# Row scores of the second layer spread by TensorE for every pair, instead of by a 32x32 turn and a way through DRAM, with new step lists

## The chip, the core and the metric

The kernel runs on one core of a Trainium2 chip. A core has five engines with queues of their own: TensorE (PE, with its weight loads shown apart as PEld), VectorE (DVE), ScalarE (ACT), GpSimd (POOL) and SyncE (SP), which here issues nearly all DMAs. [...] The metric is the device time of one execution in microseconds; lower is better.

## The reference

128 graphs of 128 nodes with 512 features go through two layers, all in f32. The first is attention with 8 heads whose scores are weighed with the adjacency; the second is a graph attention layer whose softmax runs over the rows:

```python
h = jnp.maximum(_layernorm(x, axis=-1), 0.0)
q, k, v = (proj(Wq, bq), proj(Wk, bk), proj(Wv, bv))
scores = jnp.einsum('bhqd,bhkd->bhqk', q, k) * SCALE * (adj + adj)[:, None, :, :]
ctx = jnp.einsum('bhqk,bhkd->bhqd', jax.nn.softmax(scores, axis=-1), v)
x = x + jnp.einsum('bse,fe->bsf', ctx, Wo) + bo

h = jnp.maximum(_layernorm(x, axis=-1), 0.0)
Wh = jnp.einsum('bsi,io->bso', h, W)
e = jax.nn.leaky_relu(Wh @ a[:OUT_F, :] + jnp.swapaxes(Wh @ a[OUT_F:, :], 1, 2), negative_slope=0.2)
attention = jax.nn.softmax(jnp.where(adj > 0.5, e, -9e15), axis=1)
x = x + jax.nn.elu(jnp.einsum('bst,bto->bso', attention, Wh))
```

In the kernel the second layer works on the transposed adjacency, so that its softmax runs along the free dimension. One of the two terms of e is then a number for each partition, and the other, the row score, a number for each column, which has to stand in all 128 partitions. How this row gets there is what the change touches.

## The kernel before, in words

**Tiling.** The graphs are taken in 64 pairs p, and two pairs make a group g. The products for q, k and v are made for a group at once, all others for a pair. Every product with a 512x512 weight is done with seven block products in place of eight (PRODUCTS, as in Strassen's method); that is why sums of blocks are made on VectorE: of weights (`weight_sum`, once), of the hidden rows (`hidden_sum`, steps hs0 to hs3), of the context (cs0 to cs3) and of the gathered rows (gs0 to gs3). Every f32 matmul shows as two passes in the profile, a transpose as one.

**Steps.** The work of a pair is cut into steps with short names, a table of functions for each pair (`steps`, line 680). Nothing is reordered by a scheduler: three lists written into the kernel say which step of which pair is issued next, and each engine runs its instructions in that order. HEAD (line 577) is the start, with `name@pair`; ORDER (line 601) is run through for p = 3 to 59, with `name:lag` for the pair p - lag; TAIL (line 611) is the end, with pairs counted from the last. A step that was done, or that a pair does not have, is passed over. The steps that matter here, with engine and line:

- U1 to U11 (PE, L258): block products of q, k, v for the next group, ten for an even pair and eleven for an odd one; F (ACT, L270, L275) and A (DVE, L279) take them out of PSUM.
- sca, scb (PE, L320): scores of graph a and b of the pair, two PSUM banks each; ata0, ata1, atb0, atb1 (DVE, L327): their weighing, which frees a bank each; mx (DVE, L334), ex (ACT, L339), rc (DVE, L343), nm*a*/nm*b* 0 to 3 (ACT, L348): the softmax; fl (DVE, L355), bl and pl (SP, L359, L365): the weights are turned in 32x32 blocks, written to DRAM and fetched back with the blocks in place.
- pca, pcb (PE, L388) with the pair before: context; pea, peb (ACT, L395) take it out. o0 to o6 (PE, L299) and od (DVE, L402): output product, added to x. sh (DVE, L234) adds a constant row to x first.
- st0, st1 (DVE, L165, L166), pw (POOL, L172, L173), nm (DVE, L412, writes nmr), h20, h21 (ACT, L418): norm and relu of the second layer.
- d00, d10, d01, d11 (DVE, L425): the two score columns of each graph, sums along the rows.
- px (DVE, L439), pd (SP, L444), pv (SP, L449): the row score, see below. wm (DVE, L455), pr (ACT, L460), m1 (DVE, L464), e1 (ACT, L469), sw (DVE, L474, L475): mask, leaky relu and softmax of the second layer.
- g0, g1 (PE, L481): rows gathered with these weights; ge0, ge1 (ACT, L487) take them out; w0 to w6 (PE, L299), zc (ACT, L495), wd (DVE, L499): product with W; ez (ACT), fa, fb (DVE, L511, L515), so (SP): elu, sum and store. The last pair does this by quarters (qe, qa, qb, qs).
- t0, t1 (DVE, L165), s0 (POOL), f0 (SP), lT (SP), hd0, hd1 (DVE, L222, L224): norm and relu of the first layer, ahead of time. For the first four pairs tp0, tp1 (PE, L197) transpose the normalised rows hn (DVE, L190) instead. lx, l0, la, lt (SP) load x (twice), the adjacency and its transpose.
- W and L steps (DVE, SP): sums and loads of the weights, in two halves each; ccp, ccd, ccs, cch make the constant row c (PE, L531: 16 matmuls of one column), sup and sua the rows u (PE, L553: transposes of a column broadcast over 128 columns).

**PSUM.** All PSUM tiles come from one pool of eight banks (`ps1`, line 57). A tile gets a bank when its first matmul is issued, and this matmul waits until the last reader of the tile that had the bank is done.

**The row score before.** For pairs 0 to 61, d writes the score of graph i into column 0 of `src_sb[:, i, :]` (128 x 2 x 32, zeros elsewhere). px turns this in 32x32 blocks on VectorE, so that the scores stand in rows 0, 32, 64, 96; pd writes these rows to DRAM; pv reads them back to all partitions, into the tile w; wm works there. For pairs 62 and 63, near the end, pb (`scores1`, line 429) is used: one transpose on TensorE for each graph, with the column broadcast over 128 columns as its input, into a PSUM tile that wm reads.

Of the kernel before, what the change touches and what calls it, by code (L numbers as in the profile page):

```python
# [10 lines left out]
OP = mybir.AluOpType  # L11
# [13 lines left out]
def kernel(  # L25
# [133 lines left out]
    def row_stats(src, name, soon=False):  # L159

        mv = small.tile([P, 2, 2], F32, name=name)

        def stats(i):
            st = small.tile([P, nc.vector.BN_STATS_DIM], F32, name="st", bufs=1)
            nc.vector.bn_stats(st, src[:, i, :])  # L165
            nc.vector.bn_aggr(mv[:, i, :], st)  # L166
            if soon:
                nc.vector.tensor_scalar_add(mv[:, i, 1:2], mv[:, i, 1:2], EPS)  # L168

        def power():  # L170
# [199 lines left out]
    src_sb = const.tile([P, 2, Q], F32, name="src1")  # L370
    nc.gpsimd.memset(src_sb, 0.0)


# [35 lines left out]
    def centre1(p):  # L409
        mv = l1s[p][0]  # L410
        nmr = small.tile([P, 2], F32, name="nmr", bufs=2)
# [10 lines left out]
    def dot1(p, i, k):  # L422
        h2, ws = h1s[p]
        junk = work.tile([P, E], F32, name="junk")
        nc.vector.scalar_tensor_tensor(  # L425
            junk, h2[:, i, :], 1.0, u_sb[:, k, :], op0=OP.mult, op1=OP.mult, accum_out=ws[:, i, 1:2] if k else src_sb[:, i, 0:1]
        )

    def scores1(p):

        pb = ps1.tile([P, 2, S], F32, name="pb", tag="ps1")
        for i in range(2):
            nc.tensor.transpose(pb[:, i, :], src_sb[:, i, 0:1].to_broadcast([P, P]), ident)
        pbs[p] = pb

    def turn_scores1(p):

        wts[p] = work.tile([P, 2, S], F32, name="w", bufs=2)
        nc.vector.transpose(wts[p][:, 0, 0 : 2 * Q], src_sb.rearrange("p b q -> p (b q)"))  # L439

    def send_scores1(p):
        pbs[p] = dram.tile([2, P], F32, name="row1")
        rows = wts[p][0:P:Q, 0, 0 : 2 * Q].rearrange("j (b q) -> j b q", q=Q)
        nc.sync.dma_start(pbs[p].rearrange("b (j q) -> j b q", q=Q), rows)  # L444

    def spread_scores1(p):
        r = pbs[p]
        pbs[p] = wts[p]
        nc.sync.dma_start(wts[p].rearrange("p b s -> p (b s)"), r.rearrange("b p -> (b p)").partition_broadcast(P))  # L449

    def mask1(p):

        if p not in wts:
            wts[p] = work.tile([P, 2, S], F32, name="w", bufs=2)
# [7 lines left out]
    def maxima1(p):  # L462
        l1s[p] = small.tile([P, 2], F32, name="nmx1", bufs=2), small.tile([P, 2], F32, name="sums1", bufs=2)
# [7 lines left out]
    def normalise1(p):  # L471
        w, (_, sums) = wts[p], l1s.pop(p)
        rs = small.tile([P, 2], F32, name="rs1", bufs=1)
# [100 lines left out]
    def listed(text, mark):  # L574
# [3 lines left out]
        lx@0 lx@1 Lq1@0 Lq0@0 lx@2 Lk0@0 Lk1@0 Lv0@0 t1@-5 Lo0@0 t0@-5 pp@0 hn0@0 hn1@0 tp0@0 t0@-4 tp1@0 ev0@0 ev1@0  # L578
        t1@-4 U6@-2 Wq0@0 pp@1 Wq1@0 t1@-3 U8@-2 hn0@1 l0@-2 Wq2@0 Lv1@0 hn1@1 tp0@1 Lo1@0 U3@-1 Lw1@0 t0@-3 ev0@1 Lu@0
        Wq3@0 pp@2 tp1@1 hn1@2 U5@-1 ev1@1 hn0@2 F6@-2 Wk0@0 hs0@-3 F3@-1 U1@-2 Wk1@0 hs1@-3 hs2@-3 U10@-2 tp0@2 F10@-2  # L580
        U7@-1 t1@-2 t0@-2 U2@-1 Wv0@0 F7@-1 pp@3 Wk3@0 F1@-2 A8@-2 ev0@2 U9@-1 hn0@3 Wv1@0 hn1@3 hs3@-3 tp0@3 l0@-1
        tp1@2 Wv2@0 la@-1 U3@-2 ev1@2 Lw0@0 ev0@3 lt@0 F9@-1 tp1@3 F2@-1 ccp@0 F3@-2 ev1@3 U1@0 ccd@0 t0@-1 t1@-1 U4@-2
        Wo0@0 l0@0 s0@-1 cu10@0 U5@-2 Wv3@0 A5@-1 U4@-1 hs0@-1 U10@-1 U1@-1 F10@-1 F4@-1 ccs@0 A2@-1 cch@0 sca@0 Wk2@0
        scb@0 ata0@0 ata1@0 U6@-1 mxa@0 hs1@-1 exa2@0 U3@1 t1@0 F5@-2 exa3@0 A6@-1 U6@0 A5@-2 F1@0 Wo1@0 rca1@0 t0@0
        U9@-2 F6@0 l0@1 s0@0 exa1@0 f0@0 exa0@0 U3@0 A9@-2 nma3@0 Wo2@0 nma2@0 rca0@0 cu01@0 U10@0 nma1@0 nma0@0 hs2@-1
        F3@1 U8@0 fla@0 Ww0@0 bla@0 U8@-1 atb0@0 la@0 atb1@0 mxb@0 U5@1 A8@0 exb2@0 A9@-1 pla@0 U2@-2 exb0@0 A5@1 exb1@0
        sh@0 F10@0 U11@-1 exb3@0 rcb1@0 U7@-2 nmb3@0 A11@-1 rcb0@0 t0@1 t1@1 U2@1 F7@-2 nmb1@0 cu11@0 l0@2 s0@1 nmb2@0
        f0@1 U7@1 F3@0 lT@0 cu00@0 nmb0@0 lT@1 sca@1 A2@-2 flb@0 scb@1 pca@0 F7@1 ata0@1 blb@0 ata1@1 F2@1 U5@0 mxa@1
        hs3@-1 exa0@1 U9@1 t1@2 exa1@1 Ww2@0 plb@0 exa3@1 t0@2 U1@1 exa2@1 hd0@0 s0@2 F9@1 la@1 U4@1 l0@3 pea@0 rca0@1
# [239 lines left out]
```

## Time and profile before

| | |
|---|---|
| runs | 2363.86, 2363.51, 2363.39, 2364.44 us; median 2363.69 |
| profiled execution | 2363.86 us, its span 2362.10 us (1.76 us lie around the span) |
| TensorE clock granted, mean | 0.997 |
| busy: DVE, ACT, POOL | 2001.1, 1457.1, 256.6 us |
| DMA | 314.06 MB, 133 GB/s mean |
| two pairs in the steady part | 72.65 us (the scores' first matmul at 1012.16 and at 1084.81) |

The profile's page gives each engine's busy time and share, the span in slices, the DMA queues, the chain of work that ended last, and groups of equal instructions with mean duration and the idle time before them. Other views are asked of the trace: the waits (who waited for whom, total us, times, longest), one tile's instructions, and the instructions in order of time (start, us, engine, line, operation, output and input, count, and in brackets the idle time before and what ended it). A run of equal matmuls is shown merged; its length reaches to the modelled end of the last, which overlaps the next run.

### The profile page before, as it was taken

The numbers are of one execution on the slowest core, as the hardware profiler recorded it, in microseconds if no ns is written. First come the engines' busy times: TensorE is split into PE (matmuls) and PEld (weight loads), VectorE is DVE, ScalarE is ACT, GpSimd is POOL, SyncE is SP. The second block draws the span as 40 slices with busy tenths as digits, with TensorE's granted clock in tenths as the row PEclk, the third lists the DMA queues.
The fourth block names the chain that finished last, engine by engine and source line by source line (L and its number), as shares of the span: only waits on it lengthen the run. The fifth ranks groups of instructions, "written<-read, shape, count | busy, mean of one in ns | idle before, by whom it ended". The sixth has DMA issues, their size and how long they took to land.

```text
span 2362.1 us, 41114 instructions
## 1 busy us (share of the span) xinstructions
PE 2336.9 (99%) x14184; PEld 2065.4 (87%) x14184; DVE 2001.1 (85%) x4113; ACT 1457.1 (62%) x4815; POOL 256.6 (11%) x320
## 2 busy tenths in 40 slices
PE   9999999999999999999999999999999999999998
PEld 7888888888888888888888888888888888888886
DVE  5888888888888888888888888888888888888888
ACT  2656666666566665666666666656666565665775
POOL 1101101111101011011110111110101101110000
PEclk9999999999999999999999999999999999999999
DMA  4444454454444544434545345444454443443332
GB/s 156 142 114 148 124 151 115 125 158 126 140 133 121 150 132 135 139 114 144 148 126 150 117 123 159 125 143 130 125 148 134 132 139 113 145 147 119 117 119 94
DMA packets 267352, 314.06 MB, mean 133 GB/s; under 512 B 24200, under 2 KB 192136, under 8 KB 267144
## 3 DMA queue, kind: packets, MB, share of 16 engines
q1 hardware_dynamic: 263112, 311.31, 43.8%
q8 instruction: 112, 1.84, 0.3%
q0 software_dynamic: 1920, 0.13, 0.2%
q14 instruction: 96, 0.79, 0.1%
q10 hardware_dynamic: 2112, 0.01, 0.0%
HBM read 210.51 MB, written 100.85 MB: 132 GB/s over the span
## 4 chain that ended last, share of the span: by engine, by line
PE 89%; DVE 4%; POOL 3%; ACT 3%; issue 1%; DMA 0%; POOLq 0%; SPq 0%; ACTq 0%; DVEq 0%
PE acc_a L258 26%; PE row_a L299 23%; PE acc_c L258 12%; PE row_c L299 8%; PE acc_b L258 7%; PE pc L388 5%; PE sc L320 3%; PE pg L481 3%; POOL mv L173 2%; ACT h L418 2%; DVE st L165 2%; POOL mv L172 1%; DVE x L402 1%; DVE v L279 1%; ACT gT L487 1%
## 5 line engine op out<-in xcount | busy, mean ns | idle before, releaser
L339 ACT ACTIVATE at<-at,nmx 128x128 f32<-128x128 f32 x1024 | 396.1, 391 | 18.0 <-DVE nmx L334 17.9
L299 PE MATMUL row_a<-wo,cxT 128*128 128x256 f32 x1280 | 328.4, 379 | 0.3 <-DVE cxT L153 0.3
L348 ACT ACTIVATE at<-at,rs 128x128 f32<-128x128 f32 x1024 | 323.6, 392 | 3.8 <-DVE rs L343 3.7
L299 PE MATMUL row_a<-w,gT 128*128 128x256 f32 x1280 | 319.4, 380 | 2.9 <-DVE z L499 1.7
L172 POOL TENSOR_SCALAR mv<-mv 128x2 f32<-128x2 f32 x124 | 79.2, 639 | 2031.1 <-DVE mv L166 2008.8
L299 PEld LDWEIGHTS row_a<-w,gT 128*128 128x128 f32 x1280 | 242.3, 190 | 37.9 <-DVE z L499 2.6
L299 PEld LDWEIGHTS row_a<-wo,cxT 128*128 128x128 f32 x1280 | 242.6, 190 | 34.3 <-DVE cxT L153 0.6
L402 DVE TENSOR_TENSOR x<-row_a,x 128x256 f32<-128x256 f32 x320 | 135.0, 422 | 147.3 <-PE row_a L299 144.7
L495 ACT COPY z<-row_a 128x256 f32<-128x256 f32 x256 | 94.4, 369 | 210.9 <-PE row_a L299 210.8
L275 ACT ACTIVATE kT<-acc_a,bk 128x256 f32<-128x256 f32 x256 | 106.5, 467 | 176.9 <-PE acc_a L258 173.7
L327 DVE SCALAR_TENSOR_TENSOR at<-sc,adj 128x512 f32<-128x512 f32 x256 | 165.0, 685 | 42.4 <-PE sc L320 39.9
L339 ACT ACTIVATION_READ_ACCUMULATOR at<-at,nmx 128x1 f32 x1024 | 193.8, 189 | 0.0
L418 ACT ACTIVATE h<-x,nmr,mv 128x512 f32<-128x512 f32 x128 | 97.5, 808 | 151.0 <-DVE nmr L412 148.7
L165 DVE BATCH_NORM_STATS2 st<-x 128x6 f32<-128x512 f32 x256 | 176.0, 687 | 7.3 <-DMA x<-in_x 5.0
L275 ACT ACTIVATE qT<-acc_a,bq 128x256 f32<-128x256 f32 x256 | 106.1, 466 | 123.2 <-PE acc_a L258 123.2
L425 DVE SCALAR_TENSOR_TENSOR junk<-h,u 128x512 f32<-128x512 f32 x256 | 173.1, 676 | 0.6
L355 DVE STREAM_TRANSPOSE tr<-at 128x1024 f32<-128x1024 f32 x128 | 158.7, 1240 | 7.0 <-PE pc L388 2.7
L334 DVE TENSOR_REDUCE nmx<-at 128x8 f32<-128x1024 f32 x128 | 156.2, 1220 | 4.3
L481 PEld LDWEIGHTS pg<-w,h 128*128 128x128 f32 x1024 | 133.3, 192 | 6.6 <-ACT z L495 0.2
L388 PE MATMUL pc<-aT,v 128*64 128x128 f32 x2048 | 127.5, 277 | 11.0 <-ACT gT L487 10.9
L173 POOL TENSOR_TENSOR mv<-mv,mhalf 128x2 f32<-128x2 f32 x128 | 130.6, 1020 | 32.8 <-DVE mv L168 22.5
L481 PE MATMUL pg<-w,h 128*128 128x128 f32 x1024 | 134.1, 275 | 0.0
(130 smaller groups left out, 4863.4 us busy)
## 6 DMA issues: line engine op xcount, KB each, us to landing
blocks<-tr SPq DMA_DIRECT2D x128, 512.0 KB, 6.5
aT<-blocks SPq DMA_DIRECT2D x512, 128.0 KB, 2.9
x<-in_x SPq DMA_DIRECT2D x123, 512.0 KB, 4.8
out<-x SPq DMA_DIRECT2D x63, 512.0 KB, 4.1
hA<-in_xT SPq DMA_DIRECT2D x120, 256.0 KB, 3.6
mr<-rows SPq DMA_DIRECT2D x60, 256.0 KB, 4.1
adj<-in_adj SPq DMA_DIRECT2D x64, 128.0 KB, 4.0
adjT<-in_adjT SPq DMA_DIRECT2D x64, 128.0 KB, 3.8
```

The lines of the kernel that those rows point to most:

```text
L165: nc.vector.bn_stats(st, src[:, i, :])
L173: nc.gpsimd.tensor_tensor(mv[:, :, 1], mv[:, :, 1], mhalf.to_broadcast([P, 2]), OP.pow)
L258: nc.tensor.matmul(acc[:, m, :], lhsT, rhs, start=fresh and m == 0 and c == 0, stop=c == 1, skip_group_check=True)
L275: nc.scalar.activation(dst(t, f)[:, m, :], a[:, m, :], AF.Identity, bias=bias[:, j : j + 1])
L299: nc.tensor.matmul(acc, left[:, la, c, :], w[:, wb, c, :], start=n in (0, 3) and c == 0, stop=c == 1, skip_group_check=True)
L327: nc.vector.scalar_tensor_tensor(ats[b][0][:, k * C : (k + 1) * C, :], scs[b][k], QSCALE, adjs[p][:, i : i + 1, :].to_broadcast([P, C, S]) ...
L339: nc.scalar.activation(at[:, j, :], at[:, j, :], AF.Exp, bias=nmx[:, j : j + 1], accum_out=sums[:, j : j + 1])
L348: nc.scalar.activation(at[:, j, :], at[:, j, :], AF.Copy, scale=rs[:, j : j + 1])
L355: nc.vector.transpose(trs[b], at.rearrange("p h (j k) -> p j h k", k=Q))
L388: nc.tensor.matmul(pc[s * D : (s + 1) * D, j, :], vs[b // G][:, b % G, head * D : (head + 1) * D], aT[:, :, s * C + j, :], start=True, sto ...
L425: nc.vector.scalar_tensor_tensor(junk, h2[:, i, :], 1.0, u_sb[:, k, :], op0=OP.mult, op1=OP.mult, accum_out=ws[:, i, 1:2] if k else src_sb ...
L481: nc.tensor.matmul(pg[:, c, :], h1s[p][0][:, i, c * P : (c + 1) * P], wts[p][:, i, :], start=True, stop=True)
```

## The change

All pairs now do what the last two did: d writes both score columns into the small tile `ws`, pb makes the row of each graph by a transpose on TensorE, and wm reads it from PSUM. px, pd and pv go, with `src_sb`. The small tiles st, nmr, nmx1, sums1 and rs1, which had one or two buffers, get the pool's three. The three step lists are replaced by others: the same steps, but for px, pd, pv and pb, in another order. Among what is ordered otherwise: at the start the three loads of x come ahead of the weights' loads, the statistics of pairs 0 and 1 and of half of pair 2 ahead of the first hn, and all four transposes of pairs 0 and 1 ahead of the first product; in ORDER ge1 stands ahead of h20 and h21, st1 after fb, and g0 and g1 between products o of the pair after.

```diff
         def stats(i):
-            st = small.tile([P, nc.vector.BN_STATS_DIM], F32, name="st", bufs=1)
+            st = small.tile([P, nc.vector.BN_STATS_DIM], F32, name="st")
...
-    src_sb = const.tile([P, 2, Q], F32, name="src1")
-    nc.gpsimd.memset(src_sb, 0.0)
...
-        nmr = small.tile([P, 2], F32, name="nmr", bufs=2)
+        nmr = small.tile([P, 2], F32, name="nmr")
...
         nc.vector.scalar_tensor_tensor(
-            junk, h2[:, i, :], 1.0, u_sb[:, k, :], op0=OP.mult, op1=OP.mult, accum_out=ws[:, i, 1:2] if k else src_sb[:, i, 0:1]
+            junk, h2[:, i, :], 1.0, u_sb[:, k, :], op0=OP.mult, op1=OP.mult, accum_out=ws[:, i, k : k + 1]
         )
 
     def scores1(p):
+        ws = h1s[p][1]
 
         pb = ps1.tile([P, 2, S], F32, name="pb", tag="ps1")
         for i in range(2):
-            nc.tensor.transpose(pb[:, i, :], src_sb[:, i, 0:1].to_broadcast([P, P]), ident)
+            nc.tensor.transpose(pb[:, i, :], ws[:, i, 0:1].to_broadcast([P, P]), ident)
         pbs[p] = pb
 
-    def turn_scores1(p):
+    def mask1(p):
 
         wts[p] = work.tile([P, 2, S], F32, name="w", bufs=2)
-        nc.vector.transpose(wts[p][:, 0, 0 : 2 * Q], src_sb.rearrange("p b q -> p (b q)"))
-
-    def send_scores1(p):
...
-    def spread_scores1(p):
...
-    def mask1(p):
-
-        if p not in wts:
-            wts[p] = work.tile([P, 2, S], F32, name="w", bufs=2)
         nc.vector.scalar_tensor_tensor(wts[p], adjTs.pop(p), 0.5, pbs.pop(p), op0=OP.is_le, op1=OP.subtract)
...
-        l1s[p] = small.tile([P, 2], F32, name="nmx1", bufs=2), small.tile([P, 2], F32, name="sums1", bufs=2)
+        l1s[p] = small.tile([P, 2], F32, name="nmx1"), small.tile([P, 2], F32, name="sums1")
...
-        rs = small.tile([P, 2], F32, name="rs1", bufs=1)
+        rs = small.tile([P, 2], F32, name="rs1")
...
     HEAD = """
-        lx@0 lx@1 Lq1@0 Lq0@0 lx@2 Lk0@0 Lk1@0 Lv0@0 t1@-5 Lo0@0 t0@-5 pp@0 hn0@0 hn1@0 tp0@0 t0@-4 tp1@0 ev0@0 ev1@0
-        t1@-4 U6@-2 Wq0@0 pp@1 Wq1@0 t1@-3 U8@-2 hn0@1 l0@-2 Wq2@0 Lv1@0 hn1@1 tp0@1 Lo1@0 U3@-1 Lw1@0 t0@-3 ev0@1 Lu@0
-        Wq3@0 pp@2 tp1@1 hn1@2 U5@-1 ev1@1 hn0@2 F6@-2 Wk0@0 hs0@-3 F3@-1 U1@-2 Wk1@0 hs1@-3 hs2@-3 U10@-2 tp0@2 F10@-2
-        U7@-1 t1@-2 t0@-2 U2@-1 Wv0@0 F7@-1 pp@3 Wk3@0 F1@-2 A8@-2 ev0@2 U9@-1 hn0@3 Wv1@0 hn1@3 hs3@-3 tp0@3 l0@-1
-        tp1@2 Wv2@0 la@-1 U3@-2 ev1@2 Lw0@0 ev0@3 lt@0 F9@-1 tp1@3 F2@-1 ccp@0 F3@-2 ev1@3 U1@0 ccd@0 t0@-1 t1@-1 U4@-2
...
+        lx@0 lx@1 lx@2 Lk0@0 Lv0@0 Lq0@0 Lv1@0 Lk1@0 t1@-5 Lq1@0 lt@0 t1@-4 t0@-5 t0@-4 pp@0 t1@-3 pp@1 hn0@0 l0@-2
+        hn1@0 tp0@0 Lw0@0 hn0@1 Lo1@0 tp1@0 hn1@1 ev0@0 Lw1@0 tp0@1 ev1@0 Lo0@0 tp1@1 la@-1 ev0@1 U2@-2 Lu@0 ev1@1 U3@-1
+        U8@-2 F3@-1 Wv0@0 t0@-3 U6@-2 Wv1@0 pp@2 hs0@-3 hs1@-3 U5@-1 Wk0@0 Wk1@0 Wq0@0 U1@-2 Wk3@0 hs2@-3 Wq1@0 U7@-1
+        F1@-2 hn0@2 hn1@2 Wq2@0 tp0@2 F7@-1 t1@-2 U3@-2 F6@-2 A2@-2 A8@-2 U10@-2 t0@-2 hs3@-3 pp@3 U9@-1 F10@-2 F3@-2
+        Ww0@0 A5@-1 U2@-1 F9@-1 hn0@3 ev0@2 hn1@3 Wv2@0 l0@-1 tp1@2 F2@-1 Wv3@0 ccp@0 Wk2@0 tp0@3 U10@-1 cu11@0 U4@-1
+        F10@-1 t1@-1 Wq3@0 tp1@3 F4@-1 U5@-2 t0@-1 ev1@2 ev0@3 l0@0 s0@-1 ev1@3 sca@0 scb@0 ata0@0 ata1@0 U8@-1 cu00@0
...
     ORDER = """
-        U1:0 fa:4 ge0:3 pw:2 hs1:1 fb:4 g1:3 nm:2 lT:0 so:4 sca:0 h20:2 scb:0 h21:2 ata0:0 ge1:3 ata1:0 pca:1 mxa:0
-        pcb:1 pea:1 d00:2 F1:0 U11:1 exa1:0 A6:1 A8:1 U2:0 exa0:0 d10:2 exa3:0 t0:0 px:2 exa2:0 gs0:3 rca0:0 w0:3 pd:2
-        A11:1 A10:8 A1:8 nma1:0 rca1:0 w1:3 gs1:3 t1:0 nma2:0 gs2:3 o0:1 s0:0 zc0:3 nma0:0 lx:1 wd1:3 U3:0 nma3:0 hs3:1
-        d01:2 fla:0 o1:1 F3:0 peb:1 w2:3 atb0:0 bla:0 atb1:0 w3:3 zc2:3 mxb:0 F2:0 la:-1 w4:3 pv:2 gs3:3 lt:2 U5:0 zc4:3
-        cs0:1 cs2:1 cs1:1 F5:0 sh:1 pla:0 exb3:0 U4:0 exb2:0 exb0:0 rcb1:0 od0:1 l0:-1 U7:0 od1:1 exb1:0 f0:-1 wd4c:3
-        F8:-8 A5:0 nmb3:0 A2:0 F4:0 U8:0 nmb2:0 A3:3 rcb0:0 d11:2 F11:-4 nmb0:0 cs3:1 nmb1:0 A7:-9 o2:1 w5:3 od2:1 wm:2
-        U6:0 A4:-4 flb:0 zc5:3 pr:2 m1:2 blb:0 hd0:0 e1:2 w6:3 F6:0 o4:1 F7:0 o3:1 od4:1 wd6:3 U9:0 od4c:1 sw:2 F9:0
-        plb:0 hd1:0 ez:3 o5:1 hs2:0 hs0:0 o6:1 od5:1 U10:0 A9:0 st0:1 od6:1 g0:2 st1:1 F10:0
+        U1:0 A9:1 F10:1 pw:2 so:4 hs2:1 A1:8 ge1:3 F8:-4 gs0:3 w0:3 nm:2 w1:3 zc0:3 sca:0 F11:1 h20:2 wd1:3 gs2:3 scb:0
+        h21:2 A4:8 ata0:0 ata1:0 pca:1 lx:1 hs1:1 pcb:1 mxa:0 pea:1 F1:0 U11:1 gs1:3 lT:0 exa1:0 A6:1 d00:2 U2:0 exa3:0
+        d10:2 exa0:0 A8:1 d01:2 exa2:0 U3:0 rca0:0 d11:2 peb:1 nma0:0 A11:1 w2:3 rca1:0 F2:0 cs0:1 cs1:1 nma1:0 w3:3
+        zc2:3 pb:2 nma2:0 U4:0 wm:2 nma3:0 cs2:1 A2:0 pr:2 gs3:3 F3:0 o0:1 fla:0 o1:1 atb0:0 bla:0 w4:3 A7:-9 A3:-1 m1:2
+        f0:0 atb1:0 lt:1 U5:0 zc4:3 mxb:0 la:0 e1:2 sh:1 o3:1 wd4c:3 pla:0 w5:3 od0:1 od1:1 U6:0 zc5:3 F5:0 A10:7 A5:0
+        exb2:0 sw:2 exb3:0 w6:3 exb0:0 rcb1:0 o2:1 wd6:3 exb1:0 cs3:1 g0:2 od2:1 nmb2:0 hs3:1 rcb0:0 nmb3:0 o4:1 fa:3
+        nmb1:0 U7:0 nmb0:0 t1:0 ge0:2 od4:1 od4c:1 g1:2 F7:0 flb:0 ez:3 o5:1 blb:0 F6:0 o6:1 od5:1 F4:0 st0:1 U9:0 t0:0
+        F9:0 od6:1 s0:0 U8:0 hd0:0 plb:0 hd1:0 U10:0 hs0:0 fb:3 st1:1 l0:-1
     TAIL = """
...
-        nmb3@-1 od2@-2 so@-4 ge1@-3 flb@-1 o4@-2 ge0@-3 o3@-2 od4@-2 blb@-1 cs3@-2 gs0@-3 o5@-2 pea@-1 gs1@-3 od4c@-2
-        lx@-1 od5@-2 o6@-2 st0@-2 w0@-3 od6@-2 st1@-2 w1@-3 plb@-1 gs2@-3 pw@-2 gs3@-3 zc0@-3 w3@-3 wd1@-3 o0@-1 lt@-1
-        nm@-2 o1@-1 sh@-1 h21@-2 w2@-3 h20@-2 d11@-2 zc2@-3 od0@-1 pcb@-1 d00@-2 d10@-2 w4@-3 peb@-1 od1@-1 cs0@-1 pb@-2
-        zc4@-3 cs1@-1 wm@-2 o2@-1 d01@-2 w5@-3 od2@-1 pr@-2 cs2@-1 o4@-1 cs3@-1 m1@-2 wd4c@-3 o3@-1 e1@-2 od4@-1 zc5@-3
...
+        nmb3@-1 w6@-4 wm@-3 nmb0@-1 od4@-2 zc5@-4 od4c@-2 pca@-1 pr@-3 wd6@-4 flb@-1 ez@-4 o5@-2 pea@-1 fa@-4 blb@-1
+        o0@-1 m1@-3 fb@-4 o1@-1 e1@-3 o6@-2 sw@-3 so@-4 od5@-2 g0@-3 od6@-2 st1@-2 plb@-1 g1@-3 ge0@-3 st0@-2 w0@-3
+        ge1@-3 pw@-2 gs0@-3 w1@-3 lt@-2 lx@-1 zc0@-3 lt@-1 nm@-2 gs2@-3 h21@-2 gs1@-3 wd1@-3 h20@-2 d11@-2 pcb@-1 d00@-2
+        w3@-3 gs3@-3 peb@-1 d10@-2 w2@-3 cs0@-1 cs1@-1 sh@-1 pb@-2 zc2@-3 w4@-3 od0@-1 od1@-1 zc4@-3 cs2@-1 o2@-1 wm@-2
...
-        if p < N - 2:
-            table.pop("pb")
-            table |= {
-                "px": lambda: turn_scores1(p), "pd": lambda: send_scores1(p), "pv": lambda: spread_scores1(p),
-            }
```

## The prediction

> **What bounds the kernel now.** I read the busy table first, then TensorE's waits, then its instructions in order of time through one steady stretch, then the few transposes that the kernel already makes.
>
> ```profile
> PE 2336.9 (99%) x14184; PEld 2065.4 (87%) x14184; DVE 2001.1 (85%) x4113; ACT 1457.1 (62%) x4815; POOL 256.6 (11%) x320
> ```
> ```profile
> PE 89%; DVE 4%; POOL 3%; ACT 3%; issue 1%; DMA 0%; POOLq 0%; SPq 0%; ACTq 0%; DVEq 0%
> ```
> TensorE (PE) is busy all the time and carries 89% of the chain that ended last. So a matmul that is added costs its full slot, VectorE work that is taken away gives nothing by itself, and the only other thing that can move the time is PE standing still. The waits of PE, longest first:
>
> ```profile
> PE pc L388 <- ACT gT L487: 10.9, 28, 0.4
> PE acc_a L258 <- DMA wq<-in_wqT: 1.9, 1, 1.9
> PE pt L197 <- DVE hn L190: 1.8, 1, 1.8
> PE row_a L299 <- DVE z L499: 1.7, 1, 1.7
> ```
> One wait comes 28 times, once in two pairs; the others are single events at the two ends. The order of time shows it in one pair of batches and not in the next:
>
> ```profile
> 1012.16 2.06 PE L320 MATMUL sc<-kT,qT 64*128 64x128 f32 x32
> 1014.61 1.97 PE L388 MATMUL pc<-aT,v 128*64 128x128 f32 x32 [0.39 <-ACT gT L487]
> ...
> 1047.84 2.06 PE L320 MATMUL sc<-kT,qT 64*128 64x128 f32 x32
> 1049.82 2.00 PE L388 MATMUL pc<-aT,v 128*64 128x128 f32 x32
> ```
> From sc to pc it is 2.45 us in the first and 1.98 in the second: the wait costs 0.47, more than the 0.39 that stands as idle, because the modelled end of the last sc matmul covers a little of it. Its cause is ScalarE's order:
>
> ```profile
> 1012.57 1.52 ACT L418 ACTIVATE h<-x,nmr,mv 128x512 f32<-128x512 f32 x2 [2.33 <-DVE nmr L412]
> 1013.99 0.56 ACT L487 COPY gT<-pg 128x512 f32<-128x512 f32 x1
> ```
> The copy ge1, which frees the PSUM bank that pc is given, stands behind the two h2 activations, and these wait for VectorE's nmr.
>
> **a. The added transposes.** Pairs 0 to 61 turn their row scores on PE now: 62 x 2 transposes. The price of one in the midst of other work is seen at pu, which is the same instruction (a column broadcast, against ident):
>
> ```profile
> 108.48 1.03 PE L299 MATMUL row_a<-wo,cxT 128*128 128x256 f32 x4
> 109.35 0.60 PE L553 MATMUL pu<-ident,ucol 128*128 128x128 f32 x4
> 109.78 1.89 PE L258 MATMUL acc_a<-wv,hA 128*128 128x256 f32 x8
> ```
> Four take 109.78 - 109.35 = 0.43 us of PE's time, 0.108 each, and the neighbours lose nothing (four row_a passes before take their usual 0.87). The shown 0.60 is start to modelled end and overlaps the next. So 62 x 2 x 0.108 = **+13.4**. Bounds: 0, if they fell into holes (there are hardly any), and 62 x 0.38 = 23.6, the shown length of the two pb together (2342.84, 0.38). I take the slot, since PE is never empty in the steady part. [...]
>
> **b. The wait that goes.** In the new ORDER ge1 comes right after so, ahead of h20 and h21, and the first pc waits for the first at evacuation (L327) in every pair. The wait on gT then ends: 28 x 0.47 = **-13.2** (bounds 0 and -13.2; I take the whole: ge1 stands behind F10 alone, whose product U10 ends 3.5 us before sc, so both copies, 0.72 and 0.47, are done some 2 us before sc).
>
> **c. What is late next in the steady part.** I laid the new ORDER out by hand with the rows' spacing (a 256-wide VectorE operation starts 0.34 after the last, 512-wide 0.60, 1024-wide 1.13, statistics 0.82; an exps step 0.77, a normalise step 0.60 on ACT; a U product 1.73, an o or w 0.87 on PE). Margins found, in an odd pair: pc after the first at evacuation: this starts 1.19 after sc (1049.03 against 1047.84), ends 0.65 later, with a 0.04 hop 1.88, and pc is due at 1.98: 0.10 to spare. o4 after od2 (its accumulator is read): 0.2. U5 after atb0: 0.5. o0 after wm (the bank of pb): 1.0. wm is the wait that the change adds on VectorE: it stands till pb is made, about 9.4 after sc, while VectorE is there at 8.0; behind it stand cs2, A2, gs3 and fla, and fla waits till 10.7 for ScalarE anyway, so nothing is lost. sw comes 2 us before g0. The blocks' way through DRAM (1.24 transposing, 2.7 to land, 1.75 to issue, 2.9 to land) ends 5 us before pcb. So nothing must be late; as 0.10 is small I take 0.03 a pair for 60 pairs, **+1.8** (bounds 0, and 13.2, a wait of today's size in its place).
>
> What else goes in the steady part is off the path: 62 STREAM_TRANSPOSE of 0.21 us on VectorE (13.3 us, covered by PE; it could not give more than the 4% of the chain that is VectorE's anyway), and 124 issues on SP's queue of 0.57 and 0.45. SP waits there a good deal (205.4 us before L444), all of it ahead of loads that are used tens of us later; adjT's load lt moves up past them and lands 3.8 us after its issue, an iteration before wm. wm reads PSUM instead of SBUF: 0.414 against 0.415. The second and third buffers of the small tiles take away waits of VectorE on itself that the trace does not show; nothing.
>
> **d. The start.** Before, pair 0 alone is transposed (8.62), q follows at 11.67, and the clock is low till about 18 (granted 0.90 over the first 50 us, 1.00 over the next): the first eight q passes take 3.54 us, later ones 1.73. By 18.21 PE has done 8 transposes and 16 passes, 8 x 0.108 + 2 x 1.73 = 4.3 us of work at full rate. Now three x loads come before the weights, and VectorE makes the statistics of pairs 0, 1 and half of 2 ahead of hn: five steps of 1.01 from 5.03, hn to about 10.7. Then 16 transposes at the slow rate of the warm-up (5.38 / 24 = 0.22) last to 14.2. By 18.21 that is 1.7 of work plus 4.0 at full or 2.0 at half clock: 5.7 to 3.7, a gain of 1.4 or a loss of 0.6. Loads that land later than the 4.8 us seen add up to 0.8. The single-column product pm drops the clock for one stretch today (passes after it at 38.14 to 41.61 take 3.47 for 1.73); where it falls differently this 1.7 is saved. Sum between -3.1 and +1.4; I take **-0.5**, nearest to the row of the slow passes.
>
> **e. The end.** From the last sc (2304.84) to the last PE instruction (2356.9) PE has 43.7 us of work today and 8.4 of holes; in the new TAIL the same stretch holds 2.3 us more work (w products of earlier pairs), which may fill holes: -2.3. Against it, between flb and pcb of the last pair lie 7.0 us of PE work instead of 8.6, and the way of the blocks is 8.6 long: +1.6. The steps from o6 of the last pair on are the same but for gs3. I take **0**.
>
> **Sum.** 13.4 - 13.2 + 1.8 - 0.5 + 0 = +1.5. The profiled execution took 2363.86 (span 2362.10 and 1.76 around it), 0.17 above the median of 2363.69; 2363.86 + 1.5 = **2365.4**. About 0.2% (4.7 us) is what a measurement of this kernel can tell from no change: 2359.0 to 2368.4.
>
> **Rivals.**
> 1. *The sum above*: the price of the transposes and the vanished wait cancel; own range 2361 to 2368.4. Chance 0.52.
> 2. *Slower: VectorE's nm makes pc wait.* Before the at evacuation VectorE now runs nm, wd1 and gs2 (0.15 + 0.33 + 0.31), so if nm starts later than 0.40 after sc, pc is late. nm waits for GpSimd's pow; by my layout st1 ends 2.2 before sc in one pair of two (from 0.33 before o6 ends, VectorE runs st0, t0, od6, hd0, hd1, hs0, fb, st1: 6.8; from o6 to sc PE runs four U and two w: 8.7). From statistics to nm it is 3.05 us in the trace (1009.26 to 1012.31, with fa and fb beside it), which makes nm 0.85 after sc and pc 0.45 - 0.10 = 0.35 late: 28 x 0.35 = 9.8, in place of 1.8, 2373.4; with today's 0.47 in its place 2376.8. For it: "DVE nmr L412 <- POOL mv L173" waits 28 times today. Against it: fa and fb now lie ahead of st1, and where they do not run beside it GpSimd's two steps took 0.3 + 0.7. [...] Chance 0.34.
> 3. *Slower: the ends.* Start +1.4, end +1.6, and a single-column drop as today, with c at twice its value: +1.9 + 1.6 + 1.8 over the sum, 2370.7. Chance 0.07.
> 4. *Faster.* Start -3.1, end -2.3 and no new wait: 2363.86 + 0.2 - 5.4 = 2358.7, which is just over the line. For it: the holes at the end are there. Chance 0.07.
> That the change does not do what it says (pb in holes, a price of nothing) would need holes that the trace does not have; it is within rival 4.
>
> **Range.** Rival 1 whole, most of 2 and 3: 2361 to 2375. Faster 0.07, same 0.52, slower 0.34 + 0.07 = 0.41.
>
> **What would show it.** pb must appear 128 times with 0.22 us between its start and the next product; the row "pc <- ACT gT" must be gone from PE's waits (b); from sc to pc 1.98 in all pairs, or 2.3 in every second with VectorE named at L327 (rival 2); two pairs must take 72.6 to 72.7 us, as today (1012.16 to 1084.81 is 72.65); the first v passes must start near 14; the last sc to the last PE instruction must take 50 to 54. The prediction is wrong if a wait that I gave a margin (o4, U5, o0, g0, pcb) shows 28 or more times.

## The result, and the profile after

The changed kernel took 2367.34 us (median of 41 runs, 2366.39 to 2368.47) against 2364.00 for the kernel before (61 runs, 2359.86 to 2366.68): ratio 1.0015, 95% interval 1.0010 to 1.0019. That is 3.3 us slower, and less than the 0.2% taken as "no change". The forecast was 2365.4. The profiled execution of the kernel after took 2366.60, its span 2364.8.

The page of the kernel after, busy times and then the chain that ended last:

```profile
PE 2346.9 (99%) x14308; PEld 2066.7 (87%) x14308; DVE 2006.4 (85%) x4051; ACT 1437.5 (61%) x4815; POOL 220.4 (9%) x319
...
PE 97%; DVE 1%; ACT 1%; issue 0%; DMA 0%; POOLq 0%; SPq 0%; POOL 0%; DVEq 0%; ACTq 0%
```

PE has 124 instructions more (62 x 2 transposes), and its share of the chain went from 89% to 97%: the chain no longer leaves it through the wait on gT. TensorE's waits in the kernel after (who waited for whom, total us, times, longest):

```profile
PE pt L197 <- DVE hn L190: 5.6, 1, 5.6
PE row_a L299 <- DVE z L480: 2.1, 2, 1.9
PE row_a L299 <- ACT z L476: 1.4, 4, 0.5
PE warm L543 <- POOL ident masks.py:199: 1.4, 1, 1.4
PE pc L384 <- DMA aT<-blocks: 1.3, 1, 1.3
PE row_a L299 <- DVE x L398: 0.6, 1, 0.6
PE pc L384 <- DVE at L327: 0.4, 2, 0.2
```

The row with 28 waits is gone. What is left happens once or a few times, nearly all at the two ends. TensorE in order of time through a steady pair of the kernel after (start us, us, instruction, count):

```profile
1049.76 2.06 PE L320 MATMUL sc<-kT,qT 64*128 64x128 f32 x32
1051.74 1.97 PE L384 MATMUL pc<-aT,v 128*64 128x128 f32 x32
...
1060.65 0.38 PE L430 MATMUL pb<-ident,ws 128*128 128x128 f32 x2
1060.87 1.46 PE L258 MATMUL acc_c<-wv,hS 128*128 128x256 f32 x6
```

From sc to pc it is 1.98, as in the pairs that had no wait before, and from the start of pb to the next product 0.22. The next sc but one starts at 1122.37, so two pairs take 72.61; before it was 72.65. Something of 0.43 was added to two pairs and something of 0.47 taken away, and the sum cannot be seen. The runs have to show the two terms singly.

### The profile page after: what moved, and what is told of

Its sections match the earlier page's. It is cut to its first block, busy times and chain, and to the rows that moved or that the text cites. A ratio compares the mean times of both kernels' runs of the same rounds, so it can differ in the third digit from the quotient of the medians.

```text
span 2364.8 us, 41034 instructions
## 1 busy us (share of the span) xinstructions
PE 2346.9 (99%) x14308; PEld 2066.7 (87%) x14308; DVE 2006.4 (85%) x4051; ACT 1437.5 (61%) x4815; POOL 220.4 (9%) x319
## 4 chain that ended last, share of the span: by engine, by line
PE 97%; DVE 1%; ACT 1%; issue 0%; DMA 0%; POOLq 0%; SPq 0%; POOL 0%; DVEq 0%; ACTq 0%
PE acc_a L258 28%; PE row_a L299 23%; PE acc_c L258 14%; PE row_c L299 9%; PE acc_b L258 7%; PE sc L320 5%; PE pc L384 5%; PE pg L462 5%; PE pb L430 1%; PE pt L197 0%; DVE st L165 0%; DMA x<-in_x 0%; PE pm L512 0%; DVE x L398 0%; ACT z L476 0%
## 5 line engine op out<-in xcount | busy, mean ns | idle before, releaser
L299 PE MATMUL row_a<-w,gT 128*128 128x256 f32 x1280 | 319.6, 380 | 3.5 <-DVE z L480 2.1
L299 PE MATMUL row_a<-wo,cxT 128*128 128x256 f32 x1280 | 319.6, 380 | 0.7 <-DVE x L398 0.6
L299 PEld LDWEIGHTS row_a<-w,gT 128*128 128x128 f32 x1280 | 241.7, 190 | 38.7 <-DVE z L480 3.1
L299 PEld LDWEIGHTS row_a<-wo,cxT 128*128 128x128 f32 x1280 | 233.9, 190 | 28.7 <-DVE x L398 1.0
L172 POOL TENSOR_SCALAR mv<-mv 128x2 f32<-128x2 f32 x124 | 28.9, 233 | 2065.7 <-DVE mv L166 2031.3
L173 POOL TENSOR_TENSOR mv<-mv,mhalf 128x2 f32<-128x2 f32 x128 | 144.9, 1132 | 37.8 <-DVE mv L168 27.5
L320 PEld LDWEIGHTS sc<-kT,qT 64*128 64x128 f32 x2048 | 119.9, 188 | 22.2 <-issue 21.4
L320 PE MATMUL sc<-kT,qT 64*128 64x128 f32 x2048 | 133.1, 279 | 0.1
```

Of the source, the lines that this page charges most:

```text
L299: nc.tensor.matmul(acc, left[:, la, c, :], w[:, wb, c, :], start=n in (0, 3) and c == 0, stop=c == 1, skip_group_check=True)
L320: nc.tensor.matmul(sc[s][:, j, :], qT[r, j, cols], kT[r, j, cols], start=True, stop=True)
```

## The experiments

Theory A is the prediction's own: PE is full, so an added transpose and a vanished wait both count in full, and here they cancel. Its rivals: B, neither matters and the 3.3 us are made at the ends; C, the gain is in what is taken off VectorE and SP. The later runs are about the ends. All times are medians; the kernel before ran beside each on the same chip (2364.05, 2363.96 and 2364.54 in the three groups).

### The wait alone

In ORDER of the kernel before:

```diff
-        U1:0 fa:4 ge0:3 pw:2 hs1:1 fb:4 g1:3 nm:2 lT:0 so:4 sca:0 h20:2 scb:0 h21:2 ata0:0 ge1:3 ata1:0 pca:1 mxa:0
+        U1:0 fa:4 ge0:3 pw:2 hs1:1 fb:4 g1:3 ge1:3 nm:2 lT:0 so:4 sca:0 h20:2 scb:0 h21:2 ata0:0 ata1:0 pca:1 mxa:0
```

> The kernel before, with one step moved: in ORDER ge1 stands right behind g1, ahead of nm, h20 and h21. Nothing else differs; the row scores still go through the 32x32 turn. Theory A (PE is full, so its waits and its added work count one for one, and in the change the price of pb, 62 x 0.217, and the vanished wait, 28 x 0.47, cancel): the row 'pc <- ACT gT' goes from PE's waits, sc to pc is 1.98 in every pair, two pairs take 72.65 - 0.47 = 72.18, and the time falls by 13.2 to about 2350.8. Theory B (neither the transposes nor that wait matter, since the idle time shows up elsewhere; the 3.3 us come from the two ends): 2362 to 2366, with another wait in the place of the one that went.

Measured: 2351.62 (2349.29 to 2352.41), ratio 0.9948 [0.9936, 0.9961]. ScalarE and TensorE of this kernel in order of time, in the pair that had the wait:

```profile
1007.30 0.58 ACT L487 COPY gT<-pg 128x512 f32<-128x512 f32 x1 [2.03 <-PE pg L481]
1007.78 1.52 ACT L418 ACTIVATE h<-x,nmr,mv 128x512 f32<-128x512 f32 x2
```
```profile
1007.19 2.06 PE L320 MATMUL sc<-kT,qT 64*128 64x128 f32 x32
1009.18 1.97 PE L388 MATMUL pc<-aT,v 128*64 128x128 f32 x32
```

The copy now stands ahead of h, the bank is free by 1007.88, and pc comes 1.99 after sc. Two pairs take 72.21 (expected 72.18). One word moved in a list is worth 12.4 us. B falls. This kernel has no PSUM bank more than the kernel before, so the 28 gaps were not in need of one: the copy that frees the bank stood too late in ScalarE's queue.

### The transposes alone: doubled

In `scores1` of the kernel after:

```diff
-            nc.tensor.transpose(pb[:, i, :], ws[:, i, 0:1].to_broadcast([P, P]), ident)
+            for _ in range(2):
+                nc.tensor.transpose(pb[:, i, :], ws[:, i, 0:1].to_broadcast([P, P]), ident)
```

> The kernel after, with each transpose of pb made twice into the same tile, 4 in place of 2 for a pair; the second writes the same numbers over the first. Theory A: from the start of pb to the next product 0.43 in place of 0.22, two pairs take 72.61 + 0.43 = 73.04, the time rises by 64 x 2 x 0.108 = 13.8 to about 2381. Theory B (transposes in holes or overlapped with weight loads): 2367 to 2370. Above 2385 a wait would have come in too (wm later, the bank of pb held longer).

Measured: 2381.42 (2380.55 to 2383.54), 14.1 above the kernel after; expected 13.8. TensorE in order of time:

```profile
1027.98 0.60 PE L431 MATMUL pb<-ident,ws 128*128 128x128 f32 x4
1028.42 1.89 PE L258 MATMUL acc_a<-hA,wq 128*128 128x256 f32 x8
```

Four transposes are shown as 0.60 long, and the product behind them starts 0.44 after the first. Two pairs take 73.04. The 0.108 from start to start is the price; the length shown (0.27 for one, in all 128 of pb in the kernel after) overlaps what follows.

### The new lists with the old turn

The kernel after, with `src_sb`, px, pd and pv back for pairs 0 to 61 and the old buffers of the small tiles. ORDER (HEAD and TAIL alike, by single steps):

```diff
-d10:2 exa0:0 A8:1
+d10:2 px:2 pd:2 exa0:0 A8:1
-zc2:3 pb:2 nma2:0 U4:0 wm:2 nma3:0 cs2:1 A2:0 pr:2
+zc2:3 pv:2 nma2:0 U4:0 nma3:0 cs2:1 A2:0
-w4:3 A7:-9 A3:-1 m1:2 f0:0 atb1:0 lt:1 U5:0 zc4:3 mxb:0 la:0
+w4:3 A7:-9 A3:-1 f0:0 atb1:0 wm:2 pr:2 lt:1 U5:0 zc4:3 mxb:0 m1:2 la:0
```

> The new lists with the old way of the row scores: px, pd and pv behind d10 for pairs 0 to 61, wm, pr and m1 a few steps later, so that the way through DRAM has time; small tiles with their old buffers. Theory A: the lists give the vanished wait and pb is not paid: 2367.3 - 13.4 = 2354, two pairs 72.61 - 0.43 = 72.18. Theory C (the change's gain is what it takes off VectorE and off SP's queue, and pb costs little): 2367 or slower, with waits for VectorE at L327 or L398 or for DMAs on PE.

Measured: 2355.15 (2353.89 to 2356.69), 12.2 below the kernel after. The steady part does what A says: two pairs 72.17. The missing 1.2 is at this kernel's end, where its waits show "PE row_a L299 <- ACT cxT L393: 1.5, 1, 1.5" and 2.0 in place of 1.3 for the last blocks. VectorE is busy for 2016.4 in place of 2006.4 and the kernel is faster: C falls.

### The old lists with pb

The code after with the lists before; px, pd and pv out, pb in, ahead of o2 in ORDER:

```diff
-F11:-4 nmb0:0 cs3:1 nmb1:0 A7:-9 o2:1 w5:3 od2:1 wm:2
+F11:-4 nmb0:0 cs3:1 nmb1:0 A7:-9 pb:2 o2:1 w5:3 od2:1 wm:2
```

> The old lists with pb in place of px, pd and pv, put ahead of o2 (of the product two steps ahead of wm at the ends; for pair 0 pb, wm and pr behind od5); small tiles with three buffers. Theory A: the transposes are paid and the wait on gT stays: 2364.0 + 13.4 = 2377.4, two pairs 72.65 + 0.43 = 73.08, sc to pc 2.45 in one pair of two. Theory C (less work on VectorE and SP pays back): below 2373. Above 2380 the bank that pb holds makes products wait, which would show as PE waiting in front of L258 or L299 more than 28 times.

Measured: 2380.27 (2377.59 to 2381.45), 16.2 above the kernel before. TensorE's waits, first row:

```profile
PE pc L384 <- ACT gT L468: 11.5, 29, 0.4
```

The wait is there as before, 29 times for 28; two pairs take 73.11 (expected 73.08). The median is 2.8 above the 13.4 expected; the profiled execution (2381.45) shows two single events of that size together. PE waits once for 1.63 ahead of the first pair's g0 (at 138.85), since pb and wm were put late for pair 0; and at the end the clock is low for one stretch (two products start 1.60 and 1.71 apart for 0.87, at 2359.58, 2361.18 and 2362.89; from the last sc to the start of the last group of PE instructions 52.8, 2320.92 to 2373.67, for 51.2 before, 2304.84 to 2356.03), of which more below.

These four and the two kernels make a table (us):

| | turn on VectorE | pb on TensorE |
|---|---|---|
| old lists, gT late | 2364.0 | 2380.3 |
| old lists, ge1 first | 2351.6 | not run |
| new lists | 2355.2 | 2367.3 (doubled: 2381.4) |

Down the first column the wait is worth 12.4; along the rows pb costs 16.2 and 12.2. And 2355.2 against 2351.6, with neither the wait nor pb, is what the new lists cost elsewhere: 3.5 us, of which the 1.2 at its end belong to the way the old turn was put into them. With pb the cost is nearer to 2: 2351.6 + 13.4 = 2365.0 would be the empty field, an estimate, against 2367.3 measured.

### The start

HEAD of the kernel after: pair 0's transposes before the statistics of pair 1 are complete.

```diff
-t1@-5 Lq1@0 lt@0 t1@-4 t0@-5 t0@-4 pp@0 t1@-3 pp@1 hn0@0 l0@-2 hn1@0 tp0@0 Lw0@0 hn0@1 Lo1@0 tp1@0 hn1@1
+t1@-5 Lq1@0 lt@0 t0@-5 pp@0 t1@-4 hn0@0 hn1@0 tp0@0 tp1@0 t0@-4 pp@1 l0@-2 Lw0@0 hn0@1 Lo1@0 hn1@1
...
-tp1@1 la@-1
+tp1@1 t1@-3 la@-1
```

> The kernel after with another order at the start: the statistics of pair 0, then its first half of pair 1, hn and transposes of pair 0, and only then the second half of pair 1, hn and transposes of pair 1, and the statistics of pair 2's half behind them. In the kernel after, PE stands still for 5.59 ahead of the first transposes (11.81), since five statistics of 1.01 lie ahead of hn. If VectorE's order is what holds the start (theory D), the first transposes come at 8.7 to 9.3, the first product at 12.9 to 13.9 in place of 15.28, and the time falls by 1.4 to 2.4, to 2365 to 2366. If it is the clock's low stretches or the landing of the weights (theory E), the product is not earlier or runs longer at the low clock, and the time stays at 2367.

Measured: 2368.16 (nine runs, 2365.18 to 2371.30), ratio to before 1.0026 [1.0016, 1.0036]: no gain. First TensorE of this kernel, then of the kernel after:

```profile
9.07 1.97 PE L197 MATMUL pt<-ident,hn 128*128 128x128 f32 x8 [3.53 <-DVE hn L190]
11.89 1.97 PE L197 MATMUL pt<-ident,hn 128*128 128x128 f32 x8 [0.86 <-DVE hn L190]
13.65 3.62 PE L258 MATMUL acc_b<-wv,hA 128*128 128x256 f32 x8
17.07 2.26 PE L258 MATMUL acc_a<-hA,wk 128*128 128x256 f32 x8
```
```profile
11.81 3.67 PE L197 MATMUL pt<-ident,hn 128*128 128x128 f32 x16 [5.59 <-DVE hn L190]
15.28 2.14 PE L258 MATMUL acc_b<-wv,hA 128*128 128x256 f32 x8
17.25 1.89 PE L258 MATMUL acc_a<-hA,wk 128*128 128x256 f32 x8
```

The first product does come 1.63 earlier, but it runs at the low clock (3.42 from start to start in place of 1.97), and at the second product 0.18 is left. Here theory E holds: what is earlier falls into the low stretch, which was longer too (granted 0.50 from 7.57 to 17.81, in the kernel after from 8.95 to 15.77). But this profile is of the slowest of the nine runs (2371.30, mean clock 0.996), and they scatter over 6.1 us where the 41 of the kernel after lie within 2.1. The times go with the mean clock: 0.996 in the three runs of 2371.26 to 2371.30, 0.997 or 0.998 in the six of 2365.18 to 2368.19. In the median the move is worth nothing.

### The end, twice

TAIL of the kernel after, first four steps (so behind the last pair's blocks, w3 ahead of pcb, d10 and d11 exchanged in part):

```diff
-sw@-3 so@-4 od5@-2 g0@-3 od6@-2 st1@-2 plb@-1 g1@-3
+sw@-3 od5@-2 g0@-3 od6@-2 st1@-2 plb@-1 so@-4 g1@-3
-h20@-2 d11@-2 pcb@-1 d00@-2 w3@-3 gs3@-3 peb@-1 d10@-2 w2@-3
+h20@-2 d10@-2 w3@-3 pcb@-1 d00@-2 gs3@-3 peb@-1 w2@-3
-wm@-2 d01@-2
+wm@-2 d11@-2 d01@-2
```

> The kernel after with four steps moved in TAIL: the store so of pair 60 behind the four loads of the last pair's blocks on SP, w3 of pair 61 ahead of pcb of pair 63 on PE, d10 of pair 62 in the place of d11 and d11 behind wm. In the kernel after pcb waits 1.35 for these blocks and o2 then 0.61 for x. If those waits set the end (theory F), pcb waits under 0.2, from the last sc to the last PE instruction it takes 54.2 in place of 55.4, and the time falls by 1.2 to 2366. If it is the last pair's chain of steps from statistics to g0 that sets the end by itself (theory G), the 1.90 wait for z grows by as much as is won, and the time stays at 2367.

Measured: 2369.46 (nine runs, 2367.57 to 2373.58), 2.1 above the kernel after; 2367.2 in the profiled span for 2364.8. Neither F nor G. SP of this kernel, then TensorE:

```profile
2324.81 0.40 SPq L502 DMA_DIRECT2D out<-x  x1
2325.25 0.47 SPq L97 DMA_DIRECT2D adjT<-in_adjT  x1
2328.44 0.37 SPq L72 DMA_DIRECT2D x<-in_x  x1
```
```profile
2328.84 1.09 PE L384 MATMUL pc<-aT,v 128*64 128x128 f32 x16
...
2334.39 1.13 PE L299 MATMUL row_a<-wo,cxT 128*128 128x256 f32 x4 [1.80 <-DVE x L398]
```

The wait of pcb is gone, but the load of the last pair's x stands on SP till the store has gone out, since that store frees its buffer: it is issued at 2328.44, 9.84 after the first pc shown at 2318.60 in this kernel, and in the kernel after at 2325.14, 7.62 after the same pc (2317.52): 2.2 later. Then sh, od0 and od1 are late on VectorE, and o2 waits for them. Not all of the 2.4 between the profiled spans is of the end: 1.07 is there at the last sc already (2305.38 for 2304.31), 0.86 of it a single wait for blocks at 945.36. The second run moves w3 alone:

```diff
-d11@-2 pcb@-1 d00@-2 w3@-3 gs3@-3
+d11@-2 w3@-3 pcb@-1 d00@-2 gs3@-3
```

> The kernel after with one step moved in TAIL: w3 of pair 61 ahead of pcb of pair 63; so and the loads stay where they are. The wait of pcb for its blocks falls from 1.35 to about 0.5. If that wait sets the end (theory F) the stretch from the last sc to the last PE instruction falls from 55.4 to 54.5 and the time to 2366.5; if VectorE's chain from the last x load (sh, od0, od1, then o2) sets it (theory J), o2 waits 0.61 + 0.87 = 1.5 in place of 0.61, the stretch stays at 55.4 and the time at 2367.3.

Measured: 2368.48 (eleven runs, 2366.48 to 2371.97). TensorE of this kernel:

```profile
2328.07 1.09 PE L384 MATMUL pc<-aT,v 128*64 128x128 f32 x16
...
2333.13 1.13 PE L299 MATMUL row_a<-wo,cxT 128*128 128x256 f32 x4 [1.31 <-DVE x L398]
```

The wait moved from pcb (1.35 before, none now) to o2 (0.61 before, 1.31 now): from the last sc, o2 starts after 28.51 here (2304.62 to 2333.13) and after 28.50 in the kernel after (2304.31 to 2332.81). Theory J holds for this place: the load of x and VectorE's steps behind it (sh, od0, od1) set when o2 starts, and not the blocks. The stretch to the last PE instruction did not stay at 55.4, as J expected, but took 57.0; further on, from 2346.66 to 2350.07, the granted clock is 0.50, which costs about 1.7 (the last section has the rows).

Both moves, start and end, with the old turn in the new lists:

> The new lists with the old turn, together with both moves, at the start and at the end. 2355.2 was measured with the turn alone. By theories D and F together: 2355.2 - 1.9 - 1.2 = 2352; by E and G: 2355. It would have to be under 2350 to beat the kernel before with ge1 first (2351.6) by more than the measurement tells.

Measured: 2357.14 (2354.99 to 2360.10), 2.0 slower than without them. At the end its waits repeat the two runs above: pcb waits for nothing, and o2 for 2.38 in place of it; 3.42 us of half clock follow (2320.69 to 2324.11), and from the last sc to the last PE start it takes 59.55 for 56.66 without the moves. At the start the profiled execution (2355.93) did gain: the first sc is at 44.77 for 45.77, so E does not hold for it. Of the eight runs, four with a mean clock of 0.998 or 0.999 took 2354.99 to 2356.49, about as without the moves; the median is high through the four others, at 0.996 (2357.78 to 2360.10). The moves gain nothing; that they cost 2.0 by themselves is not shown.

### The clock

All profiles up to here have a stretch of low clock at the start. Seven of these ten have a second one behind pm (mean granted clock 0.93 or 0.86 over 25 to 50 us); the run with the transposes doubled and the two with the old turn in the new lists have none (1.00). The kernel before with ge1 first, and pm made wide:

```diff
-        onces["pm"] = pm = ps1.tile([P, C], F32, name="pm", tag="ps1")
+        onces["pm"] = pm = ps1.tile([P, C, P], F32, name="pm", tag="ps1")
...
-                    pm[:, j : j + 1], wo_sb[:, 2 * (c // 2) + j // 2, c % 2, ms], bv_sb[:, c : c + 1],
+                    pm[:, j, :], wo_sb[:, 2 * (c // 2) + j // 2, c % 2, ms], bv_sb[:, c : c + 1].to_broadcast([P, P]),
```

> The kernel before with ge1 first (2351.6 measured), and pm, the 32 passes of one column, made with the column broadcast over 128 columns; column 0 is used. In the trace a pass of pm takes 0.108 with one column, as one of 128 columns does, so PE's time for it stays 3.5. If the low clock behind pm (q passes of 3.6 to 3.8 for 1.73) comes from the array having nearly nothing to do in pm (theory H), the low stretch goes, the granted clock over 25 to 50 us is 1.00 in place of 0.86 to 0.93, and the time falls by 1.7 to 3.4, to 2348.2 to 2350. If it comes at that time whatever PE does (theory I): 2351.6.

Measured: 2349.12 (five runs, 2348.00 to 2353.60), 2.5 below the kernel with ge1 first. The intervals of the two ratios overlap (0.9928 to 0.9953 here, 0.9936 to 0.9961 there), so it is the traces that show the gain: the first sc comes at 48.20 for 51.08, and the spans differ by as much (2347.0 for 2349.9). Then, on top, PE kept busy at the start:

```diff
-        warm_up()
+        warm_up(42)
...
-hn0@0 hn1@0 tp0@0 t0@-4 tp1@0 ev0@0
+hn0@0 hn1@0 tp0@0 t0@-4 tp1@0 kw@0 ev0@0
```

(kw is 16 more of the warm-up's transposes.)

> As e8, and PE kept busy at the start: 42 transposes of the warm-up in place of 24, and 16 more behind the transposes of pair 0, where PE waits for wq (1.94 in the kernel before). Theory H: no low stretch between 9 and 18 either, the first eight q passes take 1.73 in place of 3.54, granted clock over 0 to 25 us above 0.95, and 1.7 to 3.4 less than e8: 2345 to 2348. Theory I: as e8, or up to 1 more where the transposes overrun the wait.

Measured: 2346.66 (five runs, 2346.46 to 2347.56), ratio 0.9928 [0.9914, 0.9941]. TensorE behind pm with one column (ge1 first), with 128 columns, and the start of the last kernel:

```profile
33.28 4.57 PE L531 MATMUL pm<-bv,wo 128*128 128x1 f32 x32
37.72 3.76 PE L258 MATMUL acc_a<-wv,hA 128*128 128x256 f32 x8
```
```profile
33.73 3.74 PE L531 MATMUL pm<-bv,wo 128*128 128x128 f32 x32
37.31 1.89 PE L258 MATMUL acc_a<-wv,hA 128*128 128x256 f32 x8
```
```profile
11.49 1.89 PE L258 MATMUL acc_a<-hA,wq 128*128 128x256 f32 x8
13.22 1.89 PE L258 MATMUL acc_b<-hA,wq 128*128 128x256 f32 x8
```

The wide pm takes 3.58 from its start to the next product, the narrow one 3.49 at full clock (in the kernel before; the 4.44 above hold the low stretch's beginning, at 35.74), and the low stretch behind it is gone. With PE busy from 1.44 on, the first products run in 1.73 at once, where the kernel before needs 3.54 and 3.00. The mean granted clock of the first 25 us is 1.00 for 0.86.

A rival is chance: three kernels had no low stretch behind a narrow pm either. In these traces the granted clock changes at times that lie whole steps of 3.41 us apart (in the kernel before at 10.94, 17.76, 38.24 and 41.66, in the kernel after at 8.95, 15.77, 39.67 and 43.08). Counted back in such steps, an estimate, the narrow pm filled 2.3 to 3.3 of one step in the seven executions with the low stretch and at most 2.1 in the three without. The wide pm filled 2.6 and 3.1 of one, and no low stretch came. So theory H holds for both runs as far as two profiles can show it. This is the fastest kernel of the study, 17.9 below the kernel before beside it: the old way of the row scores, one copy earlier, and the clock held.

## Why the prediction was right

Right in its two big terms, and in the sum partly by luck: c was taken 1.3 too high and e 2.0 too low, and the two nearly offset. The terms, against the two profiled spans (2364.8 - 2362.1 = +2.7); b, d and e in the trace after are estimates: PE's time between two matching instructions, less what its instructions take there from start to start.

| step | taken | shown |
|---|---|---|
| a. transposes | +13.4 | 0.22 a pair; doubled +14.1 for 13.8 forecast |
| b. wait on gT | -13.2 | -12.4 alone; in the after trace, standstill from pair 4 to pair 60 less by 12.7 |
| c. new waits | +1.8 | +0.5 (within the -12.7) |
| d. start | -0.5 | +0.1 |
| e. end | 0 | +2.0 |

- **a, b.** Both rows were read rightly. The price from start to start (0.108), and not the shown length, is what a transpose costs on a full PE, and the wait's price is the distance from sc to pc (0.47), not the idle time of 0.39. Alone it gave a little less, since two pairs became shorter by 0.44 (72.65 to 72.21).
- **c.** Only two events came, both in one place. VectorE and then ScalarE at the first of them, and ScalarE in a pair without one:

```profile
976.84 0.16 DVE L408 SCALAR_TENSOR_TENSOR nmr<-mv 128x2 f32<-128x2 f32 x1 [0.28 <-POOL mv L173]
977.72 0.42 DVE L480 TENSOR_TENSOR z<-row_a,z 128x256 f32<-128x256 f32 x1 [0.72 <-ACT z L476]
978.06 0.41 DVE L155 TENSOR_TENSOR gT<-gT 128x256 f32<-128x256 f32 x1
978.40 1.28 DVE L327 SCALAR_TENSOR_TENSOR at<-sc,adj 128x512 f32<-128x512 f32 x2
```
```profile
977.32 0.37 ACT L476 COPY z<-row_a 128x256 f32<-128x256 f32 x1 [2.46 <-issue]
...
1049.91 0.37 ACT L476 COPY z<-row_a 128x256 f32<-128x256 f32 x1 [2.18 <-issue]
```

  Here sc started at 976.89, nm 0.05 before it, and at comes 1.51 after it; pc comes 2.24 after sc, 0.26 late (0.19 of it shown as idle). It is not rival 2's mechanism: nm is done at 977.00, and what VectorE waits for last, 0.72 long, is ScalarE's copy of z (zc0). This copy starts 0.43 after sc here and 0.15 after it at 1049.76. In the second event (sc at 2138.89) nm is as early as in the other pairs of its kind, 0.38 ahead of sc, the copy again 0.43 after it, and pc as late. In all pairs from 4 to 59 nm starts ahead of sc, where rival 2 had it 0.85 behind. So rival 2 was right about the order (nm, wd1, gs2 ahead of at) and wrong about nm; the thin margin hangs on zc0. Why zc0 is 0.28 late twice is not shown: the profile names no wait for it.
- **The added wait.** wm waits for pb on VectorE in 60 pairs, 86.9 us in all, up to 1.8, and PE loses nothing by it, as forecast.
- **d.** About nothing came of it, and that it was taken near nothing was luck. VectorE waited 0.98 more for pair 1's rows, so the transposes came at 11.81 and the first product at 15.28, not at 10.7 and 14.2. That this cost next to nothing fits the run on the start, where what came earlier ran at the low clock.
- **e.** This is the term that was mis-sized: 0 taken, +0.6 between pair 60 and the last sc, and +1.4 from the last sc on: this stretch is 55.4 long for 52.1, past the 50 to 54 forecast, and holds 1.95 more work (eight passes and two transposes), not 2.3. The part "between flb and pcb of the last pair lie 7.0 us of PE work instead of 8.6" came as said (pcb waits 1.35), but I took it to be offset by more work in the holes. The runs showed that the place is held a second time, by the x load and VectorE behind it. With neither pb nor the wait, new lists cost 3.5 against old ones; of these, 1.2 are at the end of the kernel with the old turn. How the 0.6 before the last sc comes about was not tried.

Of rival 3 (the ends) the end came (2.0 for its 1.6), the start did not; it explains the 2 us by which the forecast missed. Rival 4 did not come. Of the signs, the first product was named for 14 and came at 15.28.

## What to carry to other kernels

On an engine that is 99% busy, read its waits by count: one that recurs every second iteration for 0.4 us was worth 12 us, and what ended it was another engine's queue order, to be mended by moving one copy. Ask of each gain in a mixed change whether it could be had without the rest: here the reordering paid for transposes (12.2 us) that a less loaded engine (VectorE, busy for 2016.4 of the 2352.1 us with the old turn) did for nothing. At the ends, a hole that is closed reopens at the next thing that is late, so follow the chain to what was issued last (there, a load held by a store that frees its buffer) before moving anything.

## What the runs showed of the hardware

- A matmul of one column takes as long as one of 128 columns here (32 passes in 3.49 us in the kernels before and after, 3.58 wide), but behind 32 of them the clock was low in seven of ten profiled executions: in the kernel before, the next eight passes take 3.47 (38.14 to 41.61) for 1.73. With the column broadcast to 128 the drop did not come in two.
- The two low stretches in the first 50 us of the kernel before are two and one of the 3.41 us steps long: granted 0.50 from 10.94 to 17.76 (6.82) and from 38.24 to 41.66 (3.42). Theory H, that the second comes from the array having nearly nothing to do in the narrow pm, agrees with the two runs with the wide one; nothing else here tests it.
- The clock came up behind transposes alone. In the last kernel PE had made 27 transposes of the warm-up and nothing else when their spacing fell from 0.213 to 0.109, at 7.2, and the first products behind the transposes ran at 1.73.
- Much of the scatter between runs goes with the clock: of the kernel before, runs at a mean of 0.999 took 2360.1 to 2362.0, at 0.997 2363.2 to 2365.3. With the array kept busy at the start and in pm, five runs lay within 1.1 us, where the 15 runs of the kernel before beside them spread over 6.9. The 41 runs of the kernel after, without any of this, lay within 2.1.
- A low stretch came where PE had not been idle all the time. In the run with w3 first, behind a wait of 1.90, two products start 1.74 and 1.71 apart for 0.87 (2346.50, 2348.24, 2349.95); in the 3.4 us ahead of them PE had one product of 0.87 and pb of 0.22. The kernel after has the same wait (2344.58) and no drop behind it, so the wait alone does not decide it. What does is not shown.
